# A planned four-layer graph kernel: the first two graphs normalised on VectorE, load times in the plan replaced by landing times, score tiles added in pairs, and two more graphs turned by DMA

## The chip, the cores and the metric

The kernel runs on one core of one Trainium2 chip. The metric is the device time of one execution in microseconds (us), given as the median of several executions. A profile is one further execution, recorded by the hardware profiler: its span runs from the first to the last instruction.

The engines are named as in the profile: PE is TensorE (PEld its weight loads), DVE is VectorE, ACT is ScalarE, POOL is GpSimd, and SP is the engine whose queue issues most DMAs.

## What is computed

There are 32 graphs of 512 nodes with 128 features each, and one 512 x 512 adjacency matrix of zeros and ones for all of them. Four layers follow one another; each normalises, applies a relu, and adds its result to `x`:

```
h = maximum(layernorm(x), 0);  x = x + L0(h)
  L0: x_h = elu(h @ Wi + bi)
      e   = sigmoid(a_tgt[:, :, None] + a_src[:, None, :] + be) * mask
      agg = einsum('bij,bjh->bih', e, x_h);  self = x_h * sum(e, axis=-1, keepdims=True)
      out = concat([elu(concat([agg, self]) @ Wn + bn), x_h]) @ Wm + bm
h = maximum(layernorm(x), 0);  x = x + L1(h)     # gated recurrence, 5 steps, each with adj @ h
h = maximum(layernorm(x), 0);  x = x + adj @ (h @ weight) + bias
h = maximum(layernorm(x), 0);  x = x + sum_k adj^k @ h @ V_k,  k = 0..3
```

## The kernel before, in words

**Tiles.** One graph is a tile of 128 partitions and 512 columns, either with nodes on the partitions (four chunks of 128) or, turned, with features on the partitions. Four graphs form a group (`G = 4`), and layer 3 works on a group at a time. A float32 product of a turned graph with a 128 x 128 weight is written as one `nc.tensor.matmul` and stands in the profile as two MATMUL instructions; a transpose of a graph is four.

**The plan sets every order.** No engine finds its own order. `op(eng, us, due, emit, reads, writes, ...)` registers a piece of work with an assumed duration `us`, an assumed time until others may use what it wrote (`result`, by default 2.5 us for SP and 0.2 to 0.25 for the others) and a due time. `Plan.order` then runs through assumed time: at each event every free engine takes the ready operation with the earliest due time. What comes out is a fixed instruction order for each engine and DMA queue; on the chip the engines then wait on semaphores. So the assumed durations decide only the order, not the time; but a changed assumption may shift the order of everything behind it.

**Two stretches.** The first call, `plan.order(end=BRANCH)` with `BRANCH = 18`, plans 18 us of assumed time. In it, whenever PE has nothing ready, it gets a small product of ones with ones (`plan.idle`, lines 301 and 302, assumed at 0.224 us), so idle slots of PE in the plan become real matmuls. Then the program branches on whether all adjacency values are exact in the PE's fast float32 format (`inexact`, L530); with these inputs the exact arm runs, and in it there are no such filler products.

**The start.** SP issues the loads in the order graph 0, graph 1, `Wi`, `bi`, four rows of the adjacency matrix, graph 2, further weights and graph 3. `layernorm` takes the moments on DVE (L474 to L477), the reciprocal root on POOL (L479), a shift on DVE (L482), and scales with relu on ACT, four instructions of 128 columns (L487). The adjacency matrix is cast on ACT (L502), compared on DVE (L504), transposed on PE (L513) and turned into the mask of layer 0 by ACT and DVE (L517, L518); ACT also keeps an exact copy (L515).

**Layer 0** (`layer0`): for the first four graphs PE transposes (L371) and ACT copies the result (L431); then the product with `Wi` (L442), `elu` (three ACT instructions, L538, L447 and L541, and two on DVE, L543 and L545), messages and scores (L568, L573, L575), the target scores spread over the partitions (L605 on PE for the first four graphs), four score tiles (tanh on ACT, L620; times the mask on DVE, L623), the aggregation on PE (L631), and the row sums of the scores. For graphs 0 and 1 the row sums are four products of ones with the four score tiles (L442, `b<-f,ones`); for all others the tiles are added by accumulating DMAs on POOL's queue (L644). Then come `Wn` (L442), a second `elu`, `Wm` (L667), and the addition to `x` (L462).

**Layer 1** (`layer1`): for the graphs of the first group, the normalised input is transposed by PE (L371) and copied by ACT; for the others `turned_back` does it: a DVE stream transpose of 32 x 32 blocks (L383), a DMA to DRAM (L385) and one back (L415). Five steps follow, with products by `u3`, `w4`, `w3`, `w5`, `u5` (L442) and by the adjacency matrix (L821).

**Layers 2 and 3** use L821, L884, L902 and L911; DVE adds the result (L923), and SP stores it (L928).

Of the kernel before, what the change touches and what calls it, by code (L numbers as in the profile page):

```python
# [16 lines left out]
P = 128  # L17
# [24 lines left out]
class Plan:  # L42
# [7 lines left out]
    def __init__(self, slots, ahead, last):  # L50
        self.ahead, self.last, self.ops, self.vals = ahead, last, [], {}
        self.free = {k: [(0.0, i) for i in range(n)] for k, n in slots.items()}
        self.until = dict.fromkeys(self.RESULT, 0.0)
        self.shared, self.now = 0.0, 0.0
        self.slack = 0.0
        self.pieces = {}
        self.idle = None
# [60 lines left out]
    def order(self, end=None):  # L118
# [34 lines left out]
        while events:  # L153
            now = heapq.heappop(events)
            if end is not None and now >= end:
                break
            for e in self.until:
                while coming[e] and coming[e][0][0] <= now:
                    _, i, o = heapq.heappop(coming[e])
                    heapq.heappush(ready[e], (o.due, i, o))  # L160
                if self.until[e] > now:
                    continue
                passed, o = [], None
                while ready[e] and o is None:
                    x = heapq.heappop(ready[e])
                    if begins(x[2], now):
                        o = x[2]
                    else:
                        passed.append(x)
                for x in passed:  # L170
                    heapq.heappush(ready[e], x)
                if o is not None and end is not None and any(
                    c.due < o.due and t < now + 0.3 * o.us for t, _, c in coming[e]
                ):
                    heapq.heappush(ready[e], (o.due, index[o], o))
                    o = None
                if o is None and e == "PE" and end is not None and self.idle.known <= now:
                    order.append(self.idle)
                    self.until[e] = now + self.idle.us
                    heapq.heappush(events, self.until[e])  # L180
                if o is None:
                    continue
                order.append(o)
                o.begun = True
                while oldest + 1 < len(by_due) and by_due[oldest].begun:
                    oldest += 1
                o.start, self.until[e] = now, now + o.us
                if o.two:
                    self.shared = self.until[e]
                for v in o.takes:  # L190
                    v.slot = self.free[v.kind].pop(self.clean(now) if v.added else 0)[1]
                    if v.kind == "b":
                        self.pieces[v.slot] = v.pieces
                o.known = self.until[e] + o.result
                heapq.heappush(events, self.until[e])
                heapq.heappush(events, o.known)
                for v in o.vals:
                    v.left -= 1
                    if not v.left and v.kind:
                        self.free[v.kind].append((o.known, v.slot))  # L200
                        self.free[v.kind].sort()
                for a in o.after:
                    if a in index:
                        a.waits -= 1
                        a.ready = max(a.ready, self.known(o, a))
                        if not a.waits:
                            heapq.heappush(coming[a.eng], (a.ready, index[a], a))
        assert end is not None or len(order) == len(left), "the plan does not end: too few buffers"
        self.now = end or 0.0
        return order  # L210
# [3 lines left out]
def tile_four_graph_layers(  # L214
# [34 lines left out]

    PACE, FIRST_PACE, LAST_PACE = 56.0, 14.0, 30.0  # L250
    BRANCH = 18.0

    T_MM, T_TR, T_NARROW, T_PASS = 0.86, 0.44, 0.224, 0.23
    T_VEC, T_COPY, T_ACT, T_DMA = 0.61, 0.5, 0.6, 0.45
# [1 line left out]
    slots = {"x": 5, "f": 36, "q": 4, "s": 8, "d": 4, "m": 8, "b": 8}  # L256
    plan = Plan(slots, ahead=60.0, last=(B - 2) * PACE)
    op = plan.op

    cpool = ctx.enter_context(tc.tile_pool(name="const", bufs=1))  # L260
    pool = ctx.enter_context(tc.tile_pool(name="slots", bufs=1))
# [23 lines left out]
    def const(name, shape, dt=F32):  # L285
        if name not in const_tiles:
            const_tiles[name] = cpool.tile(shape, dt, tag=name, name=name)
        return Val(tile=const_tiles[name])
# [21 lines left out]
        at(warm)[:, :1], at(ones)[:, :1], AF.Tanh), [ones], [warm])  # L310


    def load(v, src, due, us=0.5, to=None, earliest=0.0):
        op("SP", us, due, lambda: nc.sync.dma_start(at(v) if to is None else to(at(v)), src), [], [v],
           earliest=earliest)
        return v

    def load_const(src, shape, name, due, us=0.5, earliest=0.0):
        return load(const(name, shape), src, due, us, earliest=earliest)

    def load_column(src, name, due):
        return load_const(src.rearrange("(p o) -> p o", o=1), [P, 1], name, due, 0.4)

    X_group = [Val("x") for _ in range(NG)]
    X = [Val(whole=X_group[b // G], part=b % G) for b in range(B)]
# [1 line left out]
        v.left += 1  # L327
    plan.vals.update(dict.fromkeys([*X_group, *X]))

    def load_graph(b, due):  # L330
        op("SP", 0.65, due, lambda: nc.sync.dma_start(
            at(X[b]), x[b].rearrange("(c p) d -> p c d", p=P)),
            [], [X_group[b // G], X[b]] if b % G == 0 else [X[b]])

    load_graph(0, -9)
    load_graph(1, -9)
    Wi_sb = load_const(Wi, [P, P], "Wi_sb", -9)
    bi_sb = load_column(bi, "bi_sb", -9)
    A_nat = [Val("f") for _ in range(NC)]
    for ic in range(NC):  # L340
        load(A_nat[ic], adj[ts(ic, P), :], -8, 0.65)
    load_graph(2, -8)


    W_tok = const("W_tok", [P, P + 2])
    load(W_tok, Wn[:P], -7, to=lambda t: t[:, :P])
    load(W_tok, We.rearrange("(t p) o -> p (t o)", p=P), -7, to=lambda t: t[:, P:])
    be_sb = load_const(be.partition_broadcast(P), [P, 1], "be_sb", -7)
    Wn_sb = load_const(Wn[P:], [P, P], "Wn_sb", -6)
    bn_sb = load_column(bn, "bn_sb", -6)  # L350
    Wm_sb = load_const(Wm.rearrange("(t p) o -> p t o", p=P), [P, 2, P], "Wm_sb", -5)
    bm_bc = load_const(bm.partition_broadcast(P), [P, P], "bm_bc", -5, earliest=BRANCH)
    load_graph(3, -6)

    def scaled(v, factor, name, due):
        t = const(name, [P, 1])
# [105 lines left out]
            nc.vector.tensor_tensor(xv, xv, t, op=ALU.add)  # L462
        op("DVE", T_VEC, due, add, [X[b], p], [X[b]], two=two)

    def layernorm(b, due):

        s, h = Val("s"), Val("f")
        def stat(lo, k=1):
# [3 lines left out]
        def moments():  # L472
# [2 lines left out]
            for c in range(NC):  # L475
                nc.vector.bn_aggr(stat(PAIRS, 2)[:, c, :], stat(STATS, 6)[:, c, :])
            nc.vector.tensor_scalar(stat(VAR), stat(PAIRS, 2)[:, :, 1], EPS, None, op0=ALU.add)  # L477
        op("DVE", 1.3, due, moments, [X[b]], [s])
        op("POOL", 1.35, due, lambda: nc.gpsimd.tensor_tensor(  # L479
            stat(SCALE), stat(VAR), at(neg_half), op=ALU.pow), [s, neg_half], [s])  # L480
        mean = lambda: stat(PAIRS, 2)[:, :, 0]
        op("DVE", 0.1, due, lambda: nc.vector.scalar_tensor_tensor(  # L482
            stat(SHIFT), mean(), -1.0, stat(SCALE), op0=ALU.mult, op1=ALU.mult),
            [s], [s], two=True)
        def scale():
            for c in range(NC):
                nc.scalar.activation(  # L487
                    at(h)[:, ts(c, P)], at(X[b])[:, c, :], AF.Relu,
                    bias=stat(SHIFT)[:, c : c + 1], scale=stat(SCALE)[:, c : c + 1],
                )  # L490
        op("ACT", 1.56, due, scale, [X[b], s], [h])
        return h


# [36 lines left out]
       [p_odd], [inexact])  # L531


    def elu(p, bias, half, due, keep, scale=1.0):


        e, t, r = Val("f"), Val("f"), Val("f")
        op("ACT", T_ACT, due, lambda: nc.scalar.activation(  # L538
            at(e), at(p), AF.Exp, bias=at(bias), scale=scale), [p, bias], [e], keep=keep)
        tanh(t, p, due, half, scale / 2)  # L540
        op("ACT", T_ACT, due, lambda: nc.scalar.activation(  # L541
            at(r), at(p), AF.Relu, bias=at(bias), scale=scale), [p, bias], [r])
        op("DVE", T_VEC, due, lambda: nc.vector.scalar_tensor_tensor(  # L543
            at(t), at(e), 1.0, at(t), op0=ALU.add, op1=ALU.mult), [e, t], [t], two=True)
        op("DVE", T_VEC, due, lambda: nc.vector.scalar_tensor_tensor(  # L545
# [3 lines left out]
    def layer0(b, h, due):  # L549
        KEEP = 12  # L550
        if b < G:
            hT = copied(transposed(h, due), due)
        else:
            hT = turned_back(h, due)
            due += 6
        d = due + 6
        xhT = elu(product(Wi_sb, hT, d, blocks=b >= G), bi_sb, bi_half, d, KEEP)

        d = due + 14
        msg, ends = Val("f"), Val("s")  # L560
        for half in range(2):
            pt = Val("b")
# [17 lines left out]
            op("DVE", 0.14, d, score, [pt, be_quarter], [ends])  # L580
            op("ACT", 0.3, d, take, [pt], [msg])

        d = due + 20
        row, tgt = Val("d"), Val("f")

        flip = Val("s")
# [38 lines left out]
                [e, mask], [e], two=True)  # L625
            es.append(e)

        d = due + 30
        pn = Val("b")
        for jc in range(NC):  # L630
            op("PE", T_MM, d, lambda jc=jc: nc.tensor.matmul(  # L631
# [2 lines left out]

        if b < 2:
            ps = Val("b")
            for jc in range(NC):
                product(ones, es[jc], d, ps, start=jc == 0, stop=jc == NC - 1)
        else:
            sums = [Val("f")]  # L640
            op("SP", T_DMA, d - 10, lambda: nc.sync.dma_start(at(sums[0]), at(es[0])),
# [1 line left out]
            for e in es[1:]:  # L643
                op("POOL", 1.0, d - 10, lambda e=e: nc.gpsimd.dma_start(  # L644
                    at(sums[0]), at(e), accum_op=ALU.add), [e, sums[0]], [sums[0]],
                   two=False, result=3.0)
            high, low, ps = Val("q"), Val("q"), Val("b")
            op("ACT", T_COPY, d, lambda: nc.scalar.copy(at(high), at(sums[0])), [sums[0]], [high])
            op("DVE", T_VEC, d, lambda: nc.vector.tensor_tensor(
# [7 lines left out]
        op("DVE", T_VEC, d, lambda: nc.vector.tensor_tensor(  # L657
            at(own), at(xhT), at(ps), op=ALU.mult), [xhT, ps], [own])
        product(Wn_sb, own, d, pn, start=False)
        recv = elu(pn, bn_sb, bn_half, d + 6, 2, ALPHA / 2)  # L660

        d = due + 44
        po = bias_first(bm_bc, own, d)
        def emit():
            for c in range(NC):
# [11 lines left out]
        return max((steady - G) * PACE + (b - steady) * LAST_PACE, b * FIRST_PACE)  # L677

    def first_layer(b):
        h = layernorm(b, begin(b))  # L680
        layer0(b, h, begin(b))

    for b in range(G):
# [22 lines left out]
    def list_rest(exact, pool):  # L706
# [121 lines left out]

        def layer1(b, h, due, pace):
            tok = parts(h, due, two=True)  # L830
            if b < G:
                pt, h = transposed(h, due), Val("f")
                op("ACT", T_COPY, due, lambda h=h, pt=pt: nc.scalar.copy(
                    at(h).rearrange("p (q c i) -> p q c i", c=NC, i=32), by_qci(at(pt))),
# [163 lines left out]
```

## Time and profile before

| | us |
|---|---|
| median of 3 runs | 1678.89 (1675.96 to 1679.08) |
| the profiled execution's own time | 1678.16 |
| its span | 1676.4 |
| first PE instruction starts | 1.04 |
| last PE instruction is done (chain of waits) | 1669.58 |
| DVE and ACT busy | 1420.3 and 1130.5 |

The granted clock of PE was 0.999. In the groups of instructions a row gives line, engine, operation, tiles, count, busy time, mean ns and the idle time before it with what ended it. Durations of successive matmuls overlap in the records, since matmuls are pipelined. So the cost of one in a row of many is the distance of two starts: the four products `b<-f,ones` that start at 42.67 us are followed by the next group at 44.39 us, 1.72 us for four, 0.43 us each, while the row's mean duration is 0.59 us.

### The profile page before, as it was taken

To read this page: it belongs to the slowest core of one execution; us is meant where nothing else is said; L and a number is where in the kernel's file an instruction comes from. 1 tells how busy PE (TensorE), PEld (TensorE's weight loads), DVE (VectorE), ACT (ScalarE), POOL (GpSimd) and SP (SyncE) were. 2 spreads that over 40 slices of the span, in tenths; PEclk is the share of its full clock that TensorE was granted. 3 is DMA by queue.
4 is the path that set the end of the run, shared out by engine and by line. 5 is a ranking of instruction groups with operands and counts; after the bars stand their busy time and mean duration, and the time that the engine had idled before them with its cause. 6 is when DMAs were issued, how large, how long until landed. Compare 5 with 4: busy or idle time off the path is not lost.

```text
span 1676.4 us, 21509 instructions
## 1 busy us (share of the span) xinstructions
PE 1662.9 (99%) x6615; PEld 1073.7 (64%) x6615; DVE 1420.3 (85%) x3327; ACT 1130.5 (67%) x2145; POOL 239.6 (14%) x243
## 2 busy tenths in 40 slices
PE   9999999999999999999999999999999999999998
PEld 7555555556666666666666666666666666666797
DVE  6888999999988888889888898888999988877742
ACT  8877677876875676656676676665777767655541
POOL 2311101211111111111101111111121110000110
PEclk9999999999999999999999999999999999999999
DMA  3444424444445434444434444344554543222301
GB/s 108 114 107 138 134 88 138 121 130 115 134 113 138 120 96 127 110 122 131 121 106 111 130 127 127 107 123 109 135 138 122 138 111 103 88 64 88 93 10 53
DMA packets 284157, 188.05 MB, mean 112 GB/s; under 512 B 77312, under 2 KB 236928, under 8 KB 284032
## 3 DMA queue, kind: packets, MB, share of 16 engines
q1 hardware_dynamic: 271072, 162.98, 32.5%
q0 software_dynamic: 12960, 23.60, 8.5%
q8 instruction: 54, 0.88, 0.2%
q14 instruction: 71, 0.58, 0.1%
HBM read 82.25 MB, written 72.81 MB: 92 GB/s over the span
## 4 chain that ended last, share of the span: by engine, by line
PE 62%; DMA 2%; DVE 1%; ACT 0%; issue 0%; SPq 0%; DVEq 0%; POOLq 0%
PE b L442 27%; PE b L821 13%; PE b L911 9%; PE b L902 5%; PE b L631 3%; PE b L667 2%; PE b L884 1%; DMA f<-f 1%; PE b L568 1%; DMA m<-f 1%; PE b L654 1%; DMA f<-m 0%; DVE f L383 0%; SPq L420 0%; ACT f L620 0%
## 5 line engine op out<-in xcount | busy, mean ns | idle before, releaser
L821 PE MATMUL b<-AQ,r 128*128 128x512 f32 x1024 | 303.8, 439 | 0.0
L431 ACT COPY f<-b 128x512 f32<-128x512 f32 x360 | 207.9, 586 | 120.6 <-PE b L821 87.2
L479 POOL TENSOR_TENSOR s<-s,nhalf 128x4 f32<-128x4 f32 x128 | 154.8, 1212 | 822.0 <-DVE s L477 702.6
L821 PEld LDWEIGHTS b<-AQ,r 128*128 128x128 f32 x1024 | 192.3, 188 | 89.3 <-issue 51.5
L846 DVE TENSOR_TENSOR f<-f,b 128x512 f32<-128x512 f32 x320 | 210.9, 676 | 26.6 <-PE b L442 26.2
L911 PE MATMUL b<-r,A_r 128*128 128x512 f32 x768 | 225.0, 427 | 0.0
L383 DVE STREAM_TRANSPOSE f<-f 128x512 f32<-128x512 f32 x244 | 204.7, 843 | 21.2 <-ACT f L487 20.4
L487 ACT ACTIVATE f<-x,s 128x128 f32<-128x128 f32 x512 | 210.5, 490 | 17.4 <-DVE s L482 16.9
L447 ACT ACTIVATE f<-f,b4w 128x512 f32<-128x512 f32 x160 | 115.4, 723 | 144.1 <-DVE f L846 143.5
L911 PEld LDWEIGHTS b<-r,A_r 128*128 128x128 f32 x768 | 139.0, 189 | 46.2 <-issue 24.4
L442 PE MATMUL b<-f,u5T 128*128 128x512 f32 x320 | 163.3, 593 | 1.0 <-DVE f L853 1.0
L442 PE MATMUL b<-f,u3T 128*128 128x512 f32 x320 | 163.3, 593 | 1.0 <-DMA f<-m 1.0
L442 PE MATMUL b<-f,w4T 128*128 128x512 f32 x320 | 162.8, 592 | 0.0
L442 PE MATMUL b<-f,w3T 128*128 128x512 f32 x320 | 162.4, 592 | 0.0
L442 PE MATMUL b<-f,w5T 128*128 128x512 f32 x320 | 162.4, 592 | 0.0
L644 POOL DMA_DIRECT2D f<-f x90 | 80.7, 896 | 536.4 <-DVE f L865 58.1
L821 PE MATMUL b<-A_r,r 128*128 128x512 f32 x512 | 151.9, 438 | 0.0
L863 DVE TENSOR_TENSOR f<-f,f 128x512 f32<-128x512 f32 x160 | 109.2, 683 | 48.9 <-ACT f L447 48.4
L902 PEld LDWEIGHTS b<-V,f 128*128 128x128 f32 x1024 | 131.4, 191 | 25.6 <-issue 19.9
L447 ACT ACTIVATE f<-b,b5w 128x512 f32<-128x512 f32 x160 | 109.4, 684 | 56.0 <-PE b L442 53.5
L447 ACT ACTIVATE f<-f,b3w 128x512 f32<-128x512 f32 x160 | 114.9, 719 | 43.1 <-DVE f L846 42.2
L795 DVE TENSOR_TENSOR r<-f,r 128x512 fp32r<-128x512 f32 x192 | 130.5, 682 | 12.6 <-ACT r L791 12.4
(106 smaller groups left out, 2539.3 us busy)
## 6 DMA issues: line engine op xcount, KB each, us to landing
m<-f SPq DMA_DIRECT2D x244, 256.0 KB, 2.1
f<-m SPq DMA_DIRECT2D x184, 256.0 KB, 2.9
f<-f POOLq DMA_DIRECT2D x90, 256.0 KB, 3.6
f<-m SPq DMA_DIRECT2D x240, 64.0 KB, 2.4
x<-in_x_dram SPq DMA_DIRECT2D x32, 256.0 KB, 3.2
out_dram<-x SPq DMA_DIRECT2D x32, 256.0 KB, 2.5
f<-f SPq DMA_DIRECT2D x30, 256.0 KB, 2.3
f<-d SPq DMA_DIRECT2D x28, 256.0 KB, 5.1
```

The source lines that it names most:

```text
L383: op("DVE", us, due, lambda: nc.vector.transpose(view_out(at(blocks)), view_in(at(src))), [src], [blocks])
L431: op("ACT", us, due, lambda: nc.scalar.copy(at(t), at(src)), [src], [t])
L442: nc.tensor.matmul(to, at(w), of, start=start, stop=stop)
L447: op("ACT", us, due, lambda: nc.scalar.activation(at(dst), at(src), AF.Tanh, bias=at(bias), scale=scale), [src, bias], [dst])
L479: op("POOL", 1.35, due, lambda: nc.gpsimd.tensor_tensor(stat(SCALE), stat(VAR), at(neg_half), op=ALU.pow), [s, neg_half], [s])
L487: nc.scalar.activation(at(h)[:, ts(c, P)], at(X[b])[:, c, :], AF.Relu, bias=stat(SHIFT)[:, c : c + 1], scale=stat(SCALE)[:, c : c + 1],)
L795: op("DVE", T_VEC, due, lambda: nc.vector.tensor_tensor(part(lo), whole(), part(hi).bitcast(F32), op=ALU.subtract), [src, hi], [lo], two=two)
L821: nc.tensor.matmul(at(pa), at(part)[:, ts(jc, P)], view(at(columns)[:, jc, :]), start=jc == n == 0, stop=jc == NC - 1 and n == PARTS - 1,)
L846: op("DVE", T_VEC, d, lambda: nc.vector.tensor_tensor(at(s), at(u), at(pg), op=ALU.add), [u, pg], [s])
L863: op("DVE", T_VEC, d, lambda c=c, h=h: nc.vector.tensor_tensor(at(c), at(c), at(h), op=ALU.subtract), [c, h], [c], two=True)
L902: nc.tensor.matmul(at(pz)[:, ts(i, D)], at(hT[i])[:, ts(ic, P)], at(V[k]), start=i == 0, stop=last and i == G - 1,)
L911: nc.tensor.matmul(at(pz), at(adjT)[:, jc, ts(ic, P)], at(part), start=False, stop=jc == NC - 1 and n == PARTS - 1,)
```

## The change

Six things change.

1. For graphs 0 and 1 (`FIRST = 2`) `layernorm` is called with `relu=False`: no shift (L482) and no ACT instructions (L487); DVE subtracts the mean and multiplies by the scale, four instructions of 128 columns; the relu is applied by the ACT instruction that copies the transposed tile. The first `elu` of these graphs has its relu on DVE, from PSUM, in place of L541 on ACT. Their due times within layer 0 are multiplied by 0.6 (`pace`).
2. For graphs 0 to 3, the moments may not be planned earlier than 12 us ahead of the graph's begin (assumed times 0, 14, 28 and 42).
3. Load instructions are planned at 0.48 us of SP's time, and most get their own `result`, 2.5 to 4.8 us, in place of 2.5. The accumulating DMAs of POOL's queue get 4.6 in place of 3.0.
4. For graphs 0 and 1 DVE adds the score tiles in pairs, and PE multiplies ones with the two sums instead of with the four tiles.
5. In layer 1 only graphs 0 and 1 are transposed by PE; graphs 2 and 3 go through `turned_back`.
6. In `Plan.order` an operation's ready time is now an event of its own. The rule that an engine waits for a more urgent operation about to become ready holds while assumed time is below `careful = 18`, before it held in the first stretch, which ends at 18.

```diff
+        self.careful = 0.0
...
-                if o is not None and end is not None and any(
+                if o is not None and now < self.careful and any(
...
                             heapq.heappush(coming[a.eng], (a.ready, index[a], a))
+                            heapq.heappush(events, a.ready)
...
+    FIRST = 2
...
+    plan.careful = 18.0
...
-        op("SP", 0.65, due, lambda: nc.sync.dma_start(
+    def load_graph(b, due, result=None):
+        op("SP", 0.48, due, lambda: nc.sync.dma_start(
...
-    load_graph(0, -9)
-    load_graph(1, -9)
+    load_graph(0, -9, 2.5)
+    load_graph(1, -9, 2.9)
...
-        load(A_nat[ic], adj[ts(ic, P), :], -8, 0.65)
-    load_graph(2, -8)
+        load(A_nat[ic], adj[ts(ic, P), :], -8, 0.48, result=3.9 + 0.2 * ic)
+    load_graph(2, -8, 4.8)
...
-    load(W_tok, Wn[:P], -7, to=lambda t: t[:, :P])
+    load(W_tok, Wn[:P], -7, to=lambda t: t[:, :P], result=4.5)
...
-    be_sb = load_const(be.partition_broadcast(P), [P, 1], "be_sb", -7)
-    Wn_sb = load_const(Wn[P:], [P, P], "Wn_sb", -6)
-    bn_sb = load_column(bn, "bn_sb", -6)
+    be_sb = load_const(be.partition_broadcast(P), [P, 1], "be_sb", -7, result=4.3)
+    Wn_sb = load_const(Wn[P:], [P, P], "Wn_sb", -6, result=4.0)
+    bn_sb = load_column(bn, "bn_sb", -6, result=3.6)
...
-    load_graph(3, -6)
+    load_graph(3, -6, 3.6)
...
-        op("DVE", 1.3, due, moments, [X[b]], [s])
+        op("DVE", 1.3, due, moments, [X[b]], [s], earliest=earliest)
...
+        def normed():
+            for c in range(NC):
+                nc.vector.tensor_scalar(
+                    at(h)[:, ts(c, P)], at(X[b])[:, c, :], mean()[:, c : c + 1],
+                    stat(SCALE)[:, c : c + 1], op0=ALU.subtract, op1=ALU.mult)
+        if relu:
+            op("ACT", 1.56, due, scale, [X[b], s], [h])
+        else:
+            op("DVE", 0.9, due, normed, [X[b], s], [h])
...
+        if relu_by_vector:
+            assert scale == 1.0
+            op("DVE", T_VEC, due, lambda: nc.vector.tensor_scalar(
+                at(r), at(p), at(bias), 0.0, op0=ALU.add, op1=ALU.max), [p, bias], [r])
...
-            hT = copied(transposed(h, due), due)
+            pt, hT = transposed(h, due), Val("f")
+            op("ACT", T_COPY, due, lambda pt=pt: nc.scalar.activation(
+                at(hT), at(pt), AF.Relu if b < FIRST else AF.Copy), [pt], [hT])
...
-        d = due + 6
-        xhT = elu(product(Wi_sb, hT, d, blocks=b >= G), bi_sb, bi_half, d, KEEP)
+        pace = 0.6 if b < FIRST else 1.0
+        d = due + 6 * pace
+        xhT = elu(product(Wi_sb, hT, d, blocks=b >= G), bi_sb, bi_half, d, KEEP,
+                  relu_by_vector=b < FIRST)
...
-            for jc in range(NC):
-                product(ones, es[jc], d, ps, start=jc == 0, stop=jc == NC - 1)
+            pair = [Val("f"), Val("f")]
+            for i in range(2):
+                op("DVE", T_VEC, d - 6, lambda i=i: nc.vector.tensor_tensor(
+                    at(pair[i]), at(es[2 * i]), at(es[2 * i + 1]), op=ALU.add),
+                    [es[2 * i], es[2 * i + 1]], [pair[i]], two=True)
+            for i in range(2):
+                product(ones, pair[i], d - 1, ps, start=i == 0, stop=i == 1)
...
-                   two=False, result=3.0)
+                   two=False, result=4.6)
...
-        h = layernorm(b, begin(b))
+        h = layernorm(b, begin(b), relu=b >= FIRST, earliest=begin(b) - 12.0 if b < G else 0.0)
...
-            if b < G:
+            if b < 2:
                 pt, h = transposed(h, due), Val("f")
```

## The prediction

> **What bounds the kernel.** I read the page's busy shares first, then who PE waited for, then PE's timeline of the first 60 us, then ACT, DVE and POOL in the same stretch, then busy time by stage.
>
> ```profile
> span 1676.4 us, 21509 instructions
> PE   1662.9 (99%) x6615; PEld 1073.7 (64%) x6615; DVE 1420.3 (85%) x3327; ACT 1130.5 (67%) x2145; POOL 239.6 (14%) x243
> ```
>
> PE is busy throughout. A busy PE is modelled, so I check by starts: a float32 product of 512 columns costs 0.43 us per MATMUL, an adjacency product 0.23 (1.86 us for eight in the chain), a 128-column one 0.11. Counts by these costs from the groups by form give about 1647 us of useful matmuls and 12 us of fillers, 1659 in all. The stream runs from 1.04 to 1669.58, 1668.5 us; a tail of 6.8 us (two DVE additions, a store, its landing) follows and is not touched. So the end is PE's useful work, plus the time without useful work at the start, plus about 6 us of small waits in 1650 us. Only these three can move.
>
> PE's timeline, first 45 us (start, us, instructions):
>
> ```profile
> 1.04 9.29 PE L301 MATMUL b<-ones 128*128 128x128 f32 x62 [1.04 <-DVE ones L296]
> 10.16 1.47 PE L513 MATMUL b<-ident,f 128*128 128x128 f32 x12
> 11.47 0.60 PE L371 MATMUL b<-ident,f 128*128 128x128 f32 x4
> ...
> 13.02 1.02 PE L442 MATMUL b<-f,Wi_sb 128*128 128x512 f32 x2
> 13.88 3.51 PE L301 MATMUL b<-ones 128*128 128x128 f32 x30
> 17.22 1.06 PE L568 MATMUL b<-W_tok,f 128*128 128x130 f32 x8
> ...
> 22.02 3.70 PE L631 MATMUL b<-f,f 128*128 128x512 f32 x8 [0.65 <-DVE f L623]
> ...
> 42.67 1.88 PE L442 MATMUL b<-f,ones 128*128 128x512 f32 x4
> 44.39 0.60 PE L605 MATMUL b<-ident,s 128*128 128x128 f32 x4
> ```
>
> To 22.02 us PE did 16 L513 and 8 L371 transposes (24 x 0.11), 4 `Wi` (4 x 0.43), 8 L568 (0.90), L605 (0.44) and L525 (0.27): 6.0 us useful, so 15.0 us of fillers and waits. From there it never lacks work:
>
> ```profile
> 22.02:60.00 37.98, 37.84 (x154) 22.15 (x155) 27.64 (x78) 33.98 (x74) 8.19 (x14) 1.00 0.41 106
> 60.00:80.00 20.00, 19.37 (x79) 11.35 (x77) 19.35 (x53) 17.41 (x33) 9.63 (x11) 1.00 0.54 125
> 80.00:100.00 20.00, 20.00 (x75) 12.21 (x74) 15.74 (x36) 16.34 (x34) 4.39 (x4) 1.00 0.47 103
> ```
>
> (Columns after the length: PE, PEld, DVE, ACT, POOL busy, granted clock, DMA share, GB/s.) ACT is nearly full from 22 to 60, DVE from 60 to 80. Both matter below.
>
> **The change part by part**, against the profiled 1678.16.
>
> *Score sums in pairs.* Removed: two of four products for two graphs, 8 MATMULs x 0.43 = 3.44 us of PE. Added: four DVE additions at 0.69 (row L545, same shape), 2.8 us. They lie at 22 to 45 us, where DVE has over 6 us idle, but the sums must precede `Wn` (L442) of their graph. If that delay had no cover it would cost up to 1.4 us per graph; PE has L631 (1.7 us) to do meanwhile. **-3.44**.
>
> *Graphs 2 and 3 by DMA.* Removed: 8 transposes x 0.11 = 0.88 us of PE, two ACT copies. Added: two L383 at 1.12, two DMAs on SP and two more behind them (2.1 and 2.9 us to landing on the page), so some 6.5 us instead of about 1.3 until `u3`'s product can start. In SP's queue the waits for L383 and for the first landing hold back whatever load or store is next; SP's queue is sparse there. The adjacency product of the first step needs no turned input and covers 1.9 us; other graphs must cover the rest. Cost between 0 and 2.3 us (all the added DVE time seen by PE, around 70 us, where DVE is full); I take 0.3, since PE had 0.63 us idle in that row. **-0.88 + 0.3**.
>
> *The normalised input and the relus of graphs 0 and 1.*
>
> ```profile
> 8.14 1.64 ACT L487 ACTIVATE f<-x,s 128x128 f32<-128x128 f32 x4
> ...
> 15.23 0.69 ACT L541 ACTIVATE f<-b,bi_sb 128x512 f32<-128x512 f32 x1
> ...
> 16.28 1.65 ACT L487 ACTIVATE f<-x,s 128x128 f32<-128x128 f32 x4
> ```
>
> ACT loses 2 x 1.6 and 2 x 0.57, 4.4 us. DVE gains 2 x 0.9 (nearest row: L474, four 128-column instructions in 0.87) and 2 x 0.68 (L518, also from PSUM), and loses two L482. Graph 0's scaling waited behind two adjacency casts on ACT (7.00 to 8.14); on DVE it can follow POOL's result at about 6.2, ending near 7.1.
>
> But PE does not take it then. In the first stretch the plan's fillers occupy PE, and their number follows assumed times: before, the adjacency landed at an assumed 7.3, and (7.3 - 0.4)/0.224 = 30.8, 31 fillers, the 62 MATMULs of the row. After: load 0.48 + 2.5, moments 1.3, root 1.35, scaling 0.9 and results of 0.2 make 7.13, 30 fillers. These 60 MATMULs run at 0.15 us each, not 0.11. The row shows a granted clock of 1.00 there, yet 7 to 11 starts per us in the early and late windows. The Trainium skill, TensorE: Matmul & The Clock Gate, Part 1, says that matmuls of the first 3.4 us or so of activity run at half rate. By the granted clock the 60 fillers would end at 1.04 + 60 x 0.112 = 7.8 us, and the new chain would begin 2.4 us earlier; by the row (9.29 us for 62) and the rule they end near 10.0. I take the row: **PE's useful work still begins at 10.1**.
>
> What is gained is that graph 0 is then first, not behind twelve L513. From L371 on, by the distances of the rows before: ACT copy +0.64, `Wi` +0.91, exp +1.06, L543 +1.30 (relu beside it, on DVE), L545 +0.79, L568 +1.05, both scores +1.5 (before 1.93, behind a mask row), L605 +0.5, L620 +0.64, L623 +0.72, L631 +0.75: 9.9 us, hence 20.0; by assumed durations 9.1, hence 19.2. Against 22.02 that is 2.0 to 2.8 us. Graph 1 gains too: its scaling no longer waits for ACT until 16.28, so half of its L568 and L605 (1.3 us) should also fill slots that were fillers, +0.6. Lower bound 0 (fillers merely move). Upper bound: from 10.1 to 22.02 there are 11.9 us, 6.0 were used, and if none is wasted 5.9 is gained. **-3.0**.
>
> POOL pays something:
>
> ```profile
> 6.34 1.05 POOL L479 TENSOR_TENSOR s<-s,nhalf 128x4 f32<-128x4 f32 x1
> ...
> 11.32 1.41 POOL L479 TENSOR_TENSOR s<-s,nhalf 128x4 f32<-128x4 f32 x1 [0.29 <-DVE s L477]
> ```
>
> Graph 1's root would run while DVE scales graph 0. The skill's SBUF — State Buffer, "Who interferes with whom", speaks against it: a two-port DVE operation such as `tensor_scalar` and a GpSimd one exclude each other entirely. By the rule the root waits for up to 0.9 us; by the rows, with DVE's two-input L504 beside the second, it grew by 0.36. Either way it ends before 8.5, and PE is on fillers until 10.1: **0**.
>
> *Cover gone.* The 16 `ones` MATMULs were work that PE could do while ACT was full (20 to 45 us). With 3.44 us less and an earlier start, PE may run dry there. ACT's own 4.4 us relief, and due times at 0.6, bring graphs 0 and 1 into the PE-heavy layer 1 earlier (first L821 at 52.09), which refills it. Between 0 and 3.4; **+0.5**, nearer to the row 22.02:60, where PE had other work at hand.
>
> *Assumed times, ready events, `careful`, earliest moments.* No instruction is added; orders change everywhere. `careful` means the same stretch as before. The waits they can move are the 6 us left after 22: PE waited 2.8 us at L654 for DVE, ACT's L648 29.9 us for accumulating DMAs; 4.6 instead of 3.0 puts these later. From -2 to +2; **0**.
>
> Sum: -3.44 - 0.88 + 0.3 - 3.0 + 0.5 = -6.5, so 1671.6 for a profiled execution of 1678.16. The median of the runs is 0.7 higher: **1672.3**. A difference of 0.2%, 3.4 us, is about what a measurement of this kernel can tell from no change.
>
> **Rivals.**
>
> *Forecast*, -3.4 to -9: 1670 to 1675.4. Chance 0.60.
>
> *More is gained*: graph 1 also runs ahead of the branch and the waits shrink: -4.3 - 5.9 - 2 = -12.2, 1666.7. For it: ACT's relief and sharper due times; against it: DVE then has some 16 us of work to do by 20 us. Chance 0.21.
>
> *Cover gone, fillers stay*: the new slots are filled by fillers and ACT bounds 22 to 45. The change does not do what it says, PE's start stays put: -4.3 - 0.3 + 3.4 = -1.2, 1677.7; with part of it 1674.5 to 1679. For it: ACT at 4.9 to 5.0 of every 5 us from 20 to 40. Chance 0.15.
>
> *Slower: VectorE becomes the bound from 60 to 300 us.* It is busy 220.6 of these 240 us, 92%, and its remaining waits are dependencies. If it sets the pace there, PE's early gain is lost, and the two L383 (2.3) and what was moved to DVE (pairs, relus, scaling: 5.9) come on top as backlog: +8, less the 0.9 of transposes, 1686. It decides once PE's waits there exceed 10 us. Against it: DVE has 19 us spare there, and 19 us more before 60. Chance 0.04.
>
> **How the numbers follow.** The likeliest case gives 1672.3. The range 1667.0 to 1676.5 holds it, the nearer half of each neighbour, and leaves out about 2 in 10. Faster by over 0.2% (below 1675.5): the forecast, the larger gain and a fifth of the third case, 0.84; within: 0.12; slower 0.04.
>
> **What would show it.** In the profile after: `ones` L442 x8 instead of x16, L371 x40 instead of x48; fillers (L301) fewer than 106, the first group about 60 and ending near 10; first L371 ahead of L513; first L631 at 19 to 20; L487 x504; PE still at 99%, DVE up by about 8 us. Wrong if the first L631 stays near 22, if PE shows waits for ACT or DVE between 22 and 60 of more than 2 us, if waits for DVE grow after 60, or if the first filler group is much shorter.

## The result, and the profile after

The changed kernel takes 1673.1 us (median of 15 runs, 1671.68 to 1675.09) against 1677.69 us for the kernel before on the same chips (15 runs, 1675.96 to 1680.67). The ratio is 0.9972, 95% interval 0.9965 to 0.9979: 4.6 us faster. Forecast: 1672.3, a ratio of 0.9961. The profiled execution took 1672.72 us.

The page of the kernel after, in its first rows:

```profile
span 1670.8 us, 21509 instructions
PE 1657.3 (99%) x6603; PEld 1074.9 (64%) x6603; DVE 1427.0 (85%) x3341; ACT 1128.7 (68%) x2133; POOL 240.6 (14%) x243
```

PE has 12 MATMULs fewer: the 8 `ones` products and 8 transposes less that were announced, and 4 fillers more, where fewer were announced. DVE is up by 6.7 us (about 8 announced). PE's timeline of the kernel after:

```profile
1.04 9.15 PE L305 MATMUL b<-ones 128*128 128x128 f32 x62 [1.04 <-DVE ones L300]
10.03 0.60 PE L376 MATMUL b<-ident,f 128*128 128x128 f32 x4
...
18.66 1.28 PE L305 MATMUL b<-ones 128*128 128x128 f32 x10
19.78 0.60 PE L376 MATMUL b<-ident,f 128*128 128x128 f32 x4
20.22 0.61 PE L305 MATMUL b<-ones 128*128 128x128 f32 x4
20.66 1.88 PE L654 MATMUL b<-f,f 128*128 128x512 f32 x4
...
33.23 2.05 PE L695 MATMUL b<-Wm_sb,f 128*128 128x128 f32 x16 [1.22 <-DVE f L564]
...
77.06 2.04 PE L447 MATMUL b<-f,u3T 128*128 128x512 f32 x2 [2.41 <-DVE f L895]
...
83.18 1.05 PE L591 MATMUL b<-W_tok,f 128*128 128x130 f32 x8
```

(L305 is the filler, L376 the transpose, L654 the aggregation, L695 the product with `Wm`, L447 here that with `u3`.) Graph 0's transposes now come straight behind the first fillers, and its aggregation starts at 20.66 in place of 22.02. But graph 1's transposes start at 19.78, later than before, among fillers: 110 of them, 106 before. In the kernel before they stood here:

```profile
18.81 0.60 PE L371 MATMUL b<-ident,f 128*128 128x128 f32 x4
```

Then PE waits, which it hardly did before. Busy time by stage, after (columns as in the prediction):

```profile
22.02:60.00 37.98, 35.30 (x151) 20.78 (x150) 32.82 (x106) 34.02 (x75) 13.23 (x17) 1.00 0.30 77
60.00:80.00 20.00, 17.59 (x55) 9.56 (x54) 17.96 (x37) 14.99 (x29) 7.18 (x11) 0.92 0.61 135
80.00:100.00 20.00, 20.00 (x86) 13.37 (x86) 15.39 (x37) 15.52 (x29) 3.95 (x4) 0.99 0.57 145
100.00:1600.00 1500.00, 1499.86 (x5781) 955.74 (x5780) 1325.04 (x3076) 1036.72 (x1952) 211.07 (x198) 1.00 0.43 117
```

and the long stage before:

```profile
100.00:1600.00 1500.00, 1495.32 (x5741) 947.67 (x5739) 1320.67 (x3055) 1027.03 (x1937) 207.82 (x196) 1.00 0.43 116
```

From 20 to 100 us PE is idle for 5.1 us (1.4 before), and the granted clock falls to 0.92 between 60 and 80. From 100 to 1600 it is idle for 0.1 us (4.7 before). By the sum below, the change had lost more by 100 us than it saved up to there, and the whole gain came after that, where it adds and removes almost no work.

**Where the time went.** PE's last matmul starts at 1663.16 us (1669.63 before), 6.5 us earlier. From there to the end it takes 7.7 us, not 6.7, since at the end three additions of VectorE wait for PE instead of two. By distances of starts against the cost of each kind of matmul: useful work -4.3 us; fillers +0.4; waits up to 22 us -0.9; waits and slow clock from 22 to 100 us +6.4 (2.2, then 8.6); after 100 us from about 5 to nothing, -5 to -8, because the costs themselves are good to some 0.15%. With the last term at -8.0 these sum to -6.4, against the 6.5 us measured, and up to 100 us the changed kernel is 1.6 us behind. The last term is the least certain, since small waits are hidden in the modelled ends of matmuls.

### The profile page after: what moved, and what is told of

It reads as the page before. It is cut to its first block, busy times and chain, and to the rows that moved or that the text cites. A ratio compares the mean times of both kernels' runs of the same rounds, so it can differ in the third digit from the quotient of the medians.

```text
span 1670.8 us, 21509 instructions
## 1 busy us (share of the span) xinstructions
PE 1657.3 (99%) x6603; PEld 1074.9 (64%) x6603; DVE 1427.0 (85%) x3341; ACT 1128.7 (68%) x2133; POOL 240.6 (14%) x243
## 4 chain that ended last, share of the span: by engine, by line
PE 97%; ACT 1%; DVE 1%; issue 0%; DVEq 0%; ACTq 0%
PE b L447 44%; PE b L849 21%; PE b L939 11%; PE b L930 7%; PE b L654 6%; PE b L695 3%; PE b L912 2%; PE b L591 2%; PE b L305 1%; PE b L682 1%; ACT f L493 0%; PE b L376 0%; DVE f L388 0%; ACT f L643 0%; DVE f L891 0%
## 5 line engine op out<-in xcount | busy, mean ns | idle before, releaser
L447 PE MATMUL b<-f,u3T 128*128 128x512 f32 x320 | 164.5, 596 | 2.4 <-DVE f L895 2.4
L447 PE MATMUL b<-f,u5T 128*128 128x512 f32 x320 | 163.3, 592 | 0.0
L447 PE MATMUL b<-f,w4T 128*128 128x512 f32 x320 | 163.2, 592 | 0.0
L447 PE MATMUL b<-f,w5T 128*128 128x512 f32 x320 | 163.1, 592 | 0.0
L447 PE MATMUL b<-f,w3T 128*128 128x512 f32 x320 | 162.6, 592 | 0.0
```

What stands on the lines that cost most here:

```text
L447: nc.tensor.matmul(to, at(w), of, start=start, stop=stop)
```

## The experiments

"Changed" is the changed kernel. `Same order` means that the plan is untouched and only what an operation emits differs. Two theories stood against each other. *Work*: the prediction's own, PE's removed work arrives at the end, and the plan's new order is neutral. *Given back*: what is saved at the start is lost where PE runs dry up to 100 us, and the gain comes from order after that. All ratios are to the kernel before.

**a. Four products again** (changed, without the pair sums)

```diff
-            pair = [Val("f"), Val("f")]
...
+            for jc in range(NC):
+                product(ones, es[jc], d, ps, start=jc == 0, stop=jc == NC - 1)
```

> The changed kernel, but with four products of ones per graph again, without the pair sums (3.44 us of PE more, 2.8 us of VectorE less). If PE's work alone sets the end, it is 3.4 us slower than the changed kernel, ratio to before about 0.9993. If the products were cover in a stretch where PE runs dry anyway, PE's idle time from 20 to 80 us falls from 5.1 us to 2 or less, and the ratio stays at 0.997 to 0.998.

Measured: 1680.12 us, ratio 1.0009 (1.0001 to 1.0017), 6 us slower than the changed kernel. PE's idle time from 20 to 80 us fell to 2.7 us, but 3.0 us came between 80 and 100 and 2.0 after it, and the granted clock was 0.91 in two stretches of 20 us. More than the 3.4 us of work: the new order alone cost some 3 us, so this run can't price the products. Run f prices them.

**b. No ready events**

```diff
-                            heapq.heappush(events, a.ready)
```

> The changed kernel, but an operation's ready time is no event of the plan again. If the waits after 100 us vanished through these events, PE is idle for 3 to 5 us again between 100 and 1600 us (0.14 us in the changed kernel, 4.7 before), ratio 0.999 to 1.000. If they vanished through the 4.6 us assumed for accumulating DMAs, or by chance of order, the idle time stays under 1.5 us and the ratio at 0.997.

Measured: 1669.78 us, ratio 0.9948 (0.9936 to 0.9961). PE's idle time from 100 to 1600 us is 0.00. The events did not remove those waits. Without them the kernel is 3 us (by the medians) to 4 us (by the ratios) faster than the changed one, at the same work: PE is idle for 4.8 us from 20 to 100 us, the clock is 1.00 in every stretch there, and the end behind PE's last matmul is as short as before (6.7 us).

**c. Accumulating DMAs assumed at 3.0 us**

```diff
-                   two=False, result=4.6)
+                   two=False, result=3.0)
```

> The changed kernel, but accumulating DMAs are assumed to land after 3.0 us again, in place of 4.6. If this assumption removed the waits, PE waits for VectorE at the row-sum product (2.8 us before, 0.0 in the changed kernel) for 2 to 3 us again, and the ratio is 0.9985 to 0.9995. If the ready events did it, there is no such wait and the ratio stays at 0.997.

Measured: 1679.17 us, ratio 1.0006 (0.9995 to 1.0016). PE waited 2.5 us for VectorE at the row-sum product (L682), 0.0 in the changed kernel, 0.9 of it after 100 us; its whole idle time after 100 us was 1.8. The assumption does keep PE from that wait in this order. But the wait explains 2.5 of 6 us; from 80 to 100 us another 2.7 us were idle. The single executions lie far apart here, 1676.09 to 1684.88 us.

**d. Fewer fillers, planned as such**

```diff
-                    self.until[e] = now + self.idle.us
+                    self.until[e] = now + (0.31 if now < 6.8 else self.idle.us)
```

> The changed kernel, but fillers are assumed at 0.31 us each, not 0.224, during the first 6.8 us of assumed time, which is what they take on the chip there; some 22 in place of 31 stand ahead of the first transpose. If the fillers hold up PE, its useful work starts at 7.7 instead of 10.0 us. By PE's work alone the time falls by these 2.3 us, ratio 0.9958. If ScalarE and VectorE bound the first 50 us, only part of it arrives, 0.5 to 1.5 us, ratio 0.9963 to 0.9969, and PE's idle time from 20 to 80 us grows.

Measured: 1680.01 us, ratio 1.0006 (0.9998 to 1.0014). PE's work did start earlier (first transpose at 8.58 us, not 10.03), but its idle time from 20 to 100 us rose to 9.4 us, with a mean clock of 0.94. The earlier start was lost twice over in another order. Both theories had it faster, and both failed. Since the plan changed too, g repeats it with the order kept.

**e. The gap at 77 us filled** (same order)

```diff
+                if u3_count[0] == 4:
+                    for _ in range(10):
+                        nc.tensor.matmul(at(dst)[:, :P], at(ones), at(ones), start=True, stop=True)
```

> The changed kernel in exactly its own order; only ten products of ones with ones (2.2 us) are put ahead of the one product that PE reaches 2.4 us early (u3, at 77.06 us), into the same PSUM tile, which that product then overwrites. If the clock is lost through this gap (granted clock 0.50 from 78 to 80 us), it stays at 1.00 there and the time falls by about 1.8 us, ratio 0.996. If the low clock has another cause, nothing changes.

Measured: 1673.03 us, ratio 0.9971 (0.9958 to 0.9983), no change. The clock, changed kernel first:

```profile
34.00:36.00 2.00, 2.00 (x18) 1.76 (x17) 1.97 (x8) 2.00 (x6) 1.38 (x2) 1.00 0.05 8
...
78.00:80.00 2.00, 2.00 (x8) 1.44 (x7) 1.92 (x4) 1.29 (x3) 0.00 (x0) 0.50 0.55 102
```

and with the gap filled:

```profile
34.00:36.00 2.00, 2.00 (x11) 2.00 (x11) 1.97 (x9) 2.00 (x6) 1.48 (x2) 0.50 0.03 8
...
78.00:80.00 2.00, 1.91 (x12) 1.24 (x11) 2.00 (x5) 2.00 (x5) 0.00 (x0) 1.00 1.06 129
```

Without a gap the clock stays at 1.00 at 78 us; the gap can cause the low clock, though it doesn't in every execution (last section). But in this execution it fell to 0.50 at 34 us, behind the wait of 1.22 us at L695, which stands in the changed kernel's trace too and did no harm there. The two falls cancel in this trace (the lines of the run are numbered 7 higher):

```profile
33.60 3.50 PE L702 MATMUL b<-Wm_sb,f 128*128 128x128 f32 x16 [1.22 <-DVE f L571]
36.94 0.60 PE L376 MATMUL b<-ident,f 128*128 128x128 f32 x4
...
78.67 1.12 PE L454 MATMUL b<-f,u3T 128*128 128x512 f32 x2
...
83.27 0.94 PE L598 MATMUL b<-W_tok,f 128*128 128x130 f32 x7
```

From L702 to the transpose behind it PE took 3.34 us, not 1.88, and was then 1.8 us later than the changed kernel; at the product with `u3` it was still 1.6 us later. From there to L598 it took 4.60 us, not 6.12. So the full clock at 78 us won 1.5 us, and the fall at 34 us had lost as much. The other executions left no trace, but each has its mean granted clock, from which one fall of 3.4 us takes 0.001. Three of the six show 0.999 and took 1671.72 to 1672.22 us; three show 0.998 and took 1673.84 to 1675.45. Of the changed kernel's 15 executions, 13 show 0.998. Where the clock stayed up, the filled gap may thus be worth 1 us or more; six executions can't show it.

**f. The `ones` products done more often** (same order, PE's 3.44 us put back)

```diff
+            if w is ones and start:
+                for _ in range(2):
+                    nc.tensor.matmul(to, at(w), of, start=True, stop=True)
             nc.tensor.matmul(to, at(w), of, start=start, stop=stop)
```

> The changed kernel in exactly its own order; two products of ones are done three times each, so that PE has the removed 3.44 us of work again at the same places, around 23 and 38 us, with nothing else moved. If PE's work alone counts, 3.4 us slower, ratio 0.9993. If PE runs dry behind them anyway, up to 50 us, 0 to 1.5 us slower, ratio 0.9972 to 0.998, and PE's idle time from 20 to 80 us is smaller by what does not arrive.

Measured: 1676.01 us, ratio 0.9989 (0.9983 to 0.9996), 2.9 us slower than the changed kernel; its span is 3.5 us longer. The work arrives whole: idle time from 20 to 100 us is not smaller (6.0 against 5.1). In this order the `ones` products are not cover. They stand in front of a transpose for which ScalarE waits (below), so they lengthen the chain even while PE runs dry later. That wait of ScalarE is 2.28 us in the changed kernel, and here:

```profile
28.39 0.28 ACT L758 ACTIVATE u3T<-b 128x128 f32<-128x128 f32 x1 [3.99 <-PE b L756]
```

**g. Eight fillers not emitted** (same order)

```diff
+        filled[0] += 1
+        if filled[0] > 8:
+            nc.tensor.matmul(spare[:, :P], at(ones), at(ones), start=True, stop=True)
```

> The changed kernel in exactly its own order; the first eight of its fillers are not emitted, so that 23 stand ahead of the first transpose. If PE's start sets the end, 2 us faster, ratio 0.996. If VectorE (9.4 us busy of every 10 from 20 to 40 us) and ScalarE bound the stretch up to 80 us, 0 to 1 us faster, ratio 0.9966 to 0.9972, and PE's idle time from 20 to 80 us is larger by what does not arrive.

Measured: 1672.72 us, ratio 0.9968 (0.9956 to 0.9980), 0.4 us faster by the medians. PE with eight fillers less:

```profile
8.41 0.60 PE L380 MATMUL b<-ident,f 128*128 128x128 f32 x4
...
31.62 2.05 PE L699 MATMUL b<-Wm_sb,f 128*128 128x128 f32 x16 [1.22 <-DVE f L568]
...
81.78 1.10 PE L451 MATMUL b<-f,Wi_sb 128*128 128x512 f32 x2 [0.66 <-DMA f<-m]
...
109.83 2.14 PE L853 MATMUL b<-A_r,r 128*128 128x512 f32 x8 [1.43 <-DVE f L689]
```

The first transpose is 1.62 us earlier than in the changed kernel (10.03), L699 still 1.61 (33.23): the fillers did hold up PE. The lead lasts to 75.50 us, where PE reaches the product with `u3` 1.56 us earlier. Behind the same wait of 2.41 us the clock stays at 1.00 in this execution, so that at 80.07 us the lead is 3.1 us. Then PE waits at 81.78 for a DMA that took 6.7 us to land in the chain of waits (median on the page 2.9), and at 109.83 for VectorE; the changed kernel reaches that product at 110.56. PE's last matmul in the records is 1.0 us earlier. Of a lead of 3.1 us, 0.7 was left by 110 us.

**h. Only graph 0 normalised by VectorE** (`FIRST = 1`)

> The changed kernel with only the first graph normalised by VectorE (FIRST = 1); the second is scaled by ScalarE as before, its relus too. VectorE has 2.4 us less to do before 40 us, ScalarE 2.2 us more. If VectorE bounds the start, graph 1's first transpose (19.78 us) comes before 17, PE is idle for 1 to 2 us less from 20 to 80 us, ratio 0.9955 to 0.9965. If ScalarE bounds it, 1 to 2 us slower.

Measured: 1676.5 us, ratio 0.9990 (0.9981 to 0.9998), 3 us slower. Graph 1's first transpose starts at 19.16 us, not before 17. PE's idle time from 20 to 100 us is 4.1 us, after 100 us 2.2. Relieving VectorE did not help; PE's longest wait was for ScalarE (2.2 us, L591).

**i. The kernel before with 4.6 us for the accumulating DMAs**

> The kernel before with one number changed: accumulating DMAs are assumed to land after 4.6 us in place of 3.0. If that alone removes the waits after 100 us, PE's idle time from 100 to 1600 us falls from 4.7 us to under 1, and the time by 3 to 5 us, ratio 0.997 to 0.998, about the whole of the change's gain. If those waits are a matter of order by chance, the idle time stays at 2 us or more, ratio 0.9985 to 1.001.

Measured: 1674.84 us, ratio 0.9982 (0.9974 to 0.9990). One assumed number, no work changed, and 3 us of the change's 4.6 appear. Who PE waited for:

```profile
PE b L821 <- DVE r L795: 3.2, 1, 3.2
```

The row-sum wait of before (2.8 us) is gone. In its place stands a single wait of 3.2 us, so the idle time after 100 us fell only from 4.7 to 3.2. Neither expectation holds in full: the row-sum wait is gone with the new assumption, the other waits came from the order.

**j. No VectorE start** (`FIRST = 0`)

> The changed kernel with FIRST = 0: ScalarE normalises and does all relus, due times of layer 0 as before; planned landings, pair sums and DMA turns stay. If the VectorE start gained what I said (3.0 us), the time is 3 us longer, ratio 0.999. If what it saves at the start is lost again between 20 and 80 us, the time stays within 1 us, ratio 0.9966 to 0.9978, with PE's idle time from 20 to 80 us at 2 us or less.

Measured: 1675.33 us, ratio 0.9985 (0.9978 to 0.9992), 2.2 us slower. 74 MATMULs of fillers stand ahead of the first transpose, which starts at 12.06 (10.03), and the first aggregation at 22.49 (20.66). Of the 2.0 us, 12 fillers more account for 1.3; the rest comes from a clock that rose later in this execution (see the last section). PE's idle time from 20 to 80 us is 6.5 us: it runs dry without the VectorE start too.

**k. Graphs 2 and 3 through PE** (`if b < G` in layer 1)

> The changed kernel, but graphs 2 and 3 enter layer 1 through PE again (0.88 us of PE more, 2.3 us of VectorE less). By PE's work 0.9 us slower, ratio 0.9977. If VectorE's extra 2.3 us keep PE waiting from 60 to 100 us, 1 to 2 us faster, ratio 0.996.

Measured: 1675.97 us, ratio 0.9987 (0.9980 to 0.9994), 2.5 us slower. 0.9 us is PE's work; idle time after 100 us is 2.2 us, where the changed kernel has 0.1, in another order. VectorE's two transposes kept nobody waiting: from 20 to 80 us PE is idle for 5.1 us with or without them.

**l. No ready events, and eight fillers not emitted**

> The changed kernel without the ready events and with the first eight fillers left out, its order otherwise that of the run without ready events. Without ready events alone the ratio was 0.9948. If the fillers' 1.7 us arrive, 0.9938; if they are lost behind ScalarE and DMAs before 120 us, as when they were left out alone, 0.9943 to 0.9950.

Measured: 1668.87 us, ratio 0.9944 (0.9931 to 0.9958), faster than both kernels: 9 us under the kernel before, 4 to 5 under the changed one. Leaving out the fillers adds 0.7 us to what b gave, which is within the two intervals.

## Why the prediction was right, and which of its steps were not

The time lies in the range, 0.8 us from the forecast. That is largely luck: three terms of the sum were off by 2.5 to 8 us, with opposite signs. Without the gain after 100 us, forecast at 0, the changed kernel would have been slower than the one before. One of the prediction's own signs of being wrong came true: between 22 and 60 us PE waits for 2.5 us for ACT and DVE (L695 1.8, L753 0.7). The first aggregation, at 20.66, is neither at the 19 to 20 forecast nor near 22.

**PE's removed work, right.** -3.44 and -0.88 were forecast. Distances of starts give -4.3, and f shows that putting the 3.44 us back, with nothing else moved, costs 2.9 us by the medians and 3.5 by the spans.

**The start, half right.** The fillers ahead of the first transpose ended near 10 us, as worked out. The chain of graph 0 gained 1.4 us where 2.0 to 2.8 were expected. Graph 1 gained nothing: its scaling on VectorE ran at 18.71 us, behind the comparisons and masks, although VectorE had stood idle for 2.5 us before 12.63, waiting for graph 0's product. Graph 1's first product with `Wi` starts at 22.38 instead of 20.35, and fillers grew by 4.

```profile
12.63 0.75 DVE L557 TENSOR_SCALAR f<-b,bi_sb 128x512 f32<-128x512 f32 x1 [2.53 <-PE b L447]
...
18.71 1.10 DVE L499 TENSOR_SCALAR f<-x,s 128x128 f32<-128x128 f32 x4
```

The failing step of this term is "half of its L568 and L605 should also fill slots that were fillers": graph 1 lost time instead, and graph 0's chain gained 0.6 us or more too little. -3.0 was forecast for the term, -0.5 found (fillers and waits up to 22 us). By j, the VectorE start with its due times is worth 2.2 us in all, other order included.

**Cover gone, mis-sized, and for another reason.** +0.5 was forecast; 3.7 us more of idle time and 3.4 us at half clock came, +6.4 us by distances of starts. I had taken the `ones` products for the cover; in the new order f refutes that. What the trace shows is a chain through ScalarE. ScalarE after the change, and then the chain of waits:

```profile
23.44 0.69 ACT L552 ACTIVATE f<-b,bi_sb 128x512 f32<-128x512 f32 x1 [1.67 <-PE b L447]
24.03 0.68 ACT L452 ACTIVATE f<-b,bi_half 128x512 f32<-128x512 f32 x1
26.98 0.28 ACT L755 ACTIVATE u3T<-b 128x128 f32<-128x128 f32 x1 [2.28 <-PE b L753]
```

```profile
28.30 1.00 ACT AQ L840 x2
29.30 0.59 ACT f L552
...
33.27 2.31 ACT f L643 x4
...
40.31 3.13 ACT f L493 x8
...
47.70 2.05 PE b L695 x16
```

ScalarE stands still for 4.0 us between 21.8 and 27.0, since the next instructions in its fixed order need graph 1's late product and a weight's transpose. From 27 to 46 us it is the chain. Before, it had work in this stretch, among it the scaling of graphs 2 and 3 (L487 at 25.08 and 27.52). The stretch from 20 to 30 us, before and then after; ScalarE is the fourth engine:

```profile
20.00:30.00 10.00, 9.36 (x38) 4.95 (x37) 7.21 (x31) 9.87 (x24) 3.69 (x8) 1.00 0.53 138
```

```profile
20.00:30.00 10.00, 9.88 (x39) 5.47 (x38) 9.43 (x34) 6.05 (x13) 4.02 (x7) 1.00 0.43 116
```

Which edit caused this is open. It is none of the following three alone: idle time from 20 to 100 us stays at 5.7 us or more in a (pairs), j (VectorE start) and k (DMA turns); it is 1.4 and 1.5 us only in the two kernels with the old start, before and i. The planned landings and the bound on the moments of graphs 0 to 3 were not tried alone. The moments of graph 2 ran at 9.88 us before and at 22.77 after, which fits, but that is argued, not shown.

**Order, wrong at zero.** 0 was forecast, with -2 to +2. The idle time after 100 us fell by 4.5 us, more by distances of starts. Run i gets 3 us from one assumed number, b takes 3 to 4 us off by removing one line, c and d add 6 with no useful work changed. The range that I gave this term was too narrow by a factor of about 3. Not all of it is chance: in every variant of the changed kernel whose plan was made anew (a to d, h, j, k, l) PE is idle for 0 to 2.2 us from 100 to 1600 us, less than in i (3.2) and before (4.7). What they have in common that does this was not found. The end behind PE's last matmul, taken as untouched, grew by 0.9 us.

**The rivals.** That fillers stay and PE runs dry is what happened at the start (forecast 1677.7 for it); it was hidden by the gain behind 100 us. That VectorE becomes the bound from 60 to 300 us did not happen: PE is idle for 2.6 us there, 2.4 of it in one wait for VectorE, where the rival needed more than 10. The case of more gain is what l reaches, 1668.87, though not by the path that I gave it.

## What to carry to other kernels

When a planner writes out fixed orders, price its assumptions as an edit of their own: an emit-only change that keeps the order measures work, and any run that replans also measures a few microseconds of order. Work taken off a full engine is only won if that engine's next instruction is ready; look in its timeline for the new wait, not at its busy share. And fillers for PE are instructions in a queue: their real duration, not the assumed one, says when PE is free.

## What the runs showed of the hardware that was not expected

**The clock falls in stages of 3.41 us, after a stage that is about half idle.** In the traces here every fall to 0.50 lasts 3.41 us (one in d twice that), apart from the one at each kernel's end, and it begins a whole number of such stages after the first clock record of its trace. The stage before the fall and the fall, changed kernel first, then run e:

```profile
73.46:76.87 3.41, 1.20 (x3) 0.19 (x1) 3.38 (x6) 3.41 (x7) 0.72 (x1) 1.00 0.71 162
76.87:80.28 3.41, 3.22 (x9) 2.21 (x10) 3.04 (x6) 2.42 (x5) 0.00 (x0) 0.50 0.69 158
```

```profile
29.84:33.26 3.42, 1.78 (x13) 1.18 (x12) 2.58 (x13) 3.42 (x10) 0.22 (x1) 1.00 0.00 0
33.26:36.67 3.41, 3.07 (x14) 3.07 (x15) 2.71 (x12) 3.03 (x8) 2.49 (x2) 0.50 0.02 5
```

So PE's wait of 2.41 us put 2.21 us of idle time into one stage. In k and g the same wait falls into two stages (1.73 and 0.68 us, 1.69 and 0.72), and the clock stays at 1.00. In e the waits of 0.75 and 1.22 us leave 1.6 us idle in one stage; in the changed kernel's trace they lie in two stages, with 1.24 and 0.73 us. No fall in any of the traces begins after a stage with less than 1.6 us of idle time, and stages with up to 1.9 us passed without one. That agrees with the Trainium skill, TensorE: Matmul & The Clock Gate, Part 1, in that the observation window runs freely and in its length, but not with its idle time of about 3.4 us: about half of that was enough.

**At the start the clock reads 1.00 because it has no record.** The first clock record lies at 5.46 us before, 5.19 after and 7.20 in i; the views count the time ahead of it as 1.00. If a filler MATMUL takes 0.224 us up to the record and 0.112 us behind it, 4.42 us and 4.70 us hold 61.7 of them before, 6.16 us and 3.79 us hold 61.3 in i; there are 62 in both. So PE ran at half rate for 4.4 us before and for 6.2 us in i, where its next product starts 0.8 us later although nothing differs up to there. The prediction's reading, half rate at the start in spite of a granted clock of 1.00, is right; the 3.4 us or so that it took from the Trainium skill are shorter than what was found. So a difference of up to 0.8 us between the starts in two traces need not come from the kernel.

**VectorE and GpSimd side by side.** The prediction weighed whether GpSimd's root would wait for VectorE's scaling. DVE, then POOL, after:

```profile
6.04 1.11 DVE L499 TENSOR_SCALAR f<-x,s 128x128 f32<-128x128 f32 x4
```

```profile
6.21 1.06 POOL L484 TENSOR_TENSOR s<-s,nhalf 128x4 f32<-128x4 f32 x1
```

It took 1.06 us, about as long as graph 0's root beside VectorE's moments (1.03), so this `tensor_scalar` did not exclude it. Whether it ran in a two-port mode, of which the prediction's rule speaks, no trace here shows. Beside VectorE's two-input addition at 24.03 us the same operation took 1.40. The scaling itself took 1.11 us for four instructions, where the row chosen for it had 0.87.
